# Moving the b2 add of seven batches off TensorE, with an earlier W1 copy and a halved last store, in a one-core conditional adapter kernel

## The chip, the core and the metric

The kernel runs on one core of one Trainium2 chip. A core has five engines with an instruction queue each: TensorE (PE in the profile; its weight loads are listed as PEld), VectorE (DVE), ScalarE (ACT), GpSimd (POOL) and SyncE (SP). SyncE only issues transfers here; ScalarE issues a few as well. The engines run side by side and meet at semaphores. The metric is the device time of one execution in microseconds, the median of three runs: 309.11 us (308.94 to 309.33).

## The reference

The input x is 128 batches of 128 rows by 512 columns in float32. Each batch has a language id (0 to 8), and ten sets of parameters lie in memory. Each batch picks its own set:

```python
w1 = W1[language_ids]          # 512 x 128 for each batch
w2 = W2[language_ids]          # 128 x 512
h = jnp.einsum('bsh,bha->bsa', hidden_states, w1) + b1[language_ids][:, None, :]
h = jax.nn.relu(h)
adapted = jnp.einsum('bsa,bah->bsh', h, w2) + b2[language_ids][:, None, :]
x = hidden_states + adapted
mean = jnp.mean(x, axis=-1, keepdims=True)
var = jnp.mean(jnp.square(x - mean), axis=-1, keepdims=True)
normed = (x - mean) * jax.lax.rsqrt(var + LN_EPS)
return normed * gamma[language_ids][:, None, :] + beta[language_ids][:, None, :]
```

What this returns is added to x once more, so the result is x + normalised(x + adapted) * gamma + beta.

## The kernel before

One tile is one batch: 128 rows on the partitions, 512 columns. The work of a batch b is spread over the engines:

- TensorE: `transpose_x(b)` (line 234, four 128x128 transposes into PSUM), `down(b)` (line 257, four products with W1, printed as eight matmul records), `up(b)` (line 274, the product with W2, printed as two).
- ScalarE: `copy_xT(b)` (line 238, the transposed x out of PSUM), `relu(b)` (line 265), `stage_w1(b)` (line 225, a copy of the W1 of the batch's id out of a table in SBUF), `square(b)` (line 310, the sum of squares), `root` (line 320).
- VectorE: `residual(b)` (line 291, y + r with the row sum), `scale(b)` (line 353, subtract the mean and multiply by gamma), `finish(b)` (line 362, multiply by the reciprocal deviation and add what lies in o), and four small steps for each pair of batches (lines 298, 324, 326, 329).
- GpSimd: `add_b2(b)` (line 244, r = x + b2) and `add_beta(b)` (line 251, o = x + beta).
- SyncE: loads of x, four batches at a time (line 71), and stores of two batches (line 366).

The b2 of a batch is added in one of three ways. `b2_by_matmul` lets TensorE do it: one bf16 matmul (line 273) picks the row of b2 and writes it into PSUM ahead of the product with W2. `b2_by_vector` lets VectorE add it into PSUM (line 284) ahead of `residual`. All other batches have it from GpSimd, as r. Where TensorE or VectorE does it, `residual` reads x itself instead of r.

The order on every engine is the order in which the program is written: `keep` ties each instruction to the one before it on the same engine. The main loop runs over i; in turn i TensorE transposes batch i, multiplies `down(i - 1)` and `up(i - 2)`, and the rest works on b = i - 3.

Buffers bound how far one engine runs ahead of another. The PSUM tiles y of `up` (pool p_y) are five, so `up(b + 5)` waits for `finish(b)`. The tiles r (pool rp) are four. The tiles o hold two batches each and are five; each is free again when its store has landed. The tiles w1s (one batch's W1) are five. The transposed x in PSUM is one.

Ahead of the loop, nine matmuls on ones (`spin`) run on TensorE, then the rows of beta, gamma and b2 for all ten ids are spread over the partitions (`spread`, lines 205 to 210): 30 matmuls, each copied out of PSUM by VectorE or ScalarE.

W1 comes to a batch in three ways. Batches below FIRST (8) load it from memory by id (`load_first`, line 154). Batches from FIRST to EARLY - 1 (23) copy it out of w1e, a table in which row p * 4 + k of W1 lies on partition p; x is transposed with a matching stride. From EARLY (24) on, batches copy it out of w1, where rows k * 128 + p lie on partition p; this table is loaded by four transfers of 640 KB (`load_w1`, line 103) in turns 12, 14, 16 and 18.

The last batches (`tail`) are finished one at a time. With E = 123, GpSimd and ScalarE finish batches 123 and 124 and the left half of 125 (`by_pool`, lines 408 to 412); VectorE finishes the others (`finish_cols`, line 419). `store_last` (line 415) stores one batch; the stores of 124 and 125 are issued by ScalarE, the last one (127) by SyncE.

Of the kernel before, what the change touches and what calls it, by code (L numbers as in the profile page):

```python
# [16 lines left out]
P = 128  # L17
G = 4
EPS = 1e-5
FIRST = 8  # L20
EARLY = 24
LATE = 12
U = 2

# [2 lines left out]
def cond_resid_kernel(ctx: ExitStack, tc: tile.TileContext, x, itok, W1, b1, W2, b2, gamma, beta, out):  # L27
# [8 lines left out]
    nc = tc.nc  # L36
    B, S, H = x.shape
# [8 lines left out]
    def keep(ins):  # L46

        engine = ins.ins.engine
        if engine in last:
            tc.add_manual_dep(ins.ins, last[engine], behind, reason="kept order")  # L50
        last[engine] = ins.ins.name
        return ins
# [14 lines left out]
    E = B - 5  # L67
# [6 lines left out]
    def xb(b):  # L74
        return xs[b // G][:, b % G, :]
# [11 lines left out]
    def load_part(lo, hi):  # L87
        dst = xs[lo // G][:, lo % G : lo % G + hi - lo, :]
        keep(nc.sync.dma_start(out=dst, in_=x[lo:hi].rearrange("b s h -> s b h")))
# [11 lines left out]
    def load_w1(k):  # L101
        keep(
            nc.sync.dma_start(out=w1[:, :, k, :], in_=W1[:, k * P : (k + 1) * P, :].rearrange("l p a -> p l a"))
        )
# [28 lines left out]
    def lid(b, engine):  # L133
        g = b // G
        if (g, engine) not in lids:
            loads, vals = nc.values_load_multi_w_load_instructions(
                lang[0:1, g * G : (g + 1) * G],
                engines=[engine],
                min_val=0,
                max_val=L - 1,  # L140
                skip_runtime_bounds_check_because="clamped on the chip to 0..L-1 above",
            )
            for ins in loads:
                keep(ins)
            lids[g, engine] = vals
        return lids[g, engine][b % G]
# [4 lines left out]
    def load_first(b):  # L151
        w1s[b] = wp.tile([P, KC, A], FP, tag="w1s", name=f"w1s_{b}")
        src = W1[bass.ds(lid(b, ET.SP), 1)].rearrange("o (p k) a -> p (o k a)", k=KC)
        keep(nc.sync.dma_start(out=w1s[b].rearrange("p k a -> p (k a)"), in_=src))
# [5 lines left out]
    def load_early(lo, hi):  # L160
        dst = w1e[:, lo:hi].rearrange("p l k a -> p l (k a)")
        keep(nc.sync.dma_start(out=dst, in_=W1[lo:hi].rearrange("l (p k) a -> p l (k a)", k=KC)))
# [13 lines left out]
    xs[2] = xp.tile([P, G, H], FP, tag="x", name="x_2")  # L176
    load_part(2 * G, 2 * G + 2)
    load_early(0, 5)
    load_early(5, L)
    load_part(2 * G + 2, 3 * G)  # L180

    left = rp.tile([P, H], FP, tag="r", name="left")
# [29 lines left out]
    xT, hT, rs, os, ys, ssqs, nmeans, rstds = {}, {}, {}, {}, {}, {}, {}, {}  # L212
# [1 line left out]


    def b2_by_matmul(b):
        return b in (0, 1, 2, 3, 5, B - 1) or (b % 32 == 30 and b < E)

    def b2_by_vector(b):
        return 8 <= b < B - 8 and (b % 4 == 1 if b < 24 else b % 16 in (1, 6, 11))  # L220

    def stage_w1(b):
        w1s[b] = wp.tile([P, KC, A], FP, tag="w1s", name=f"w1s_{b}")
        src = (w1e if b < EARLY else w1).rearrange("p l k a -> p (l k a)")[:, bass.ds(lid(b, ET.Activation) * (KC * A), KC * A)]
        keep(nc.scalar.copy(w1s[b].rearrange("p k a -> p (k a)"), src))  # L225

    def transpose_x(b):
        pxs[b] = p_x.tile([P, KC, P], FP, tag="xT", name=f"pxT_{b}")
        for k in range(KC):
            if b < EARLY:  # L230
                cols = xb(b).rearrange("s (p k) -> s k p", k=KC)[:, k, :]
# [54 lines left out]
    def residual(b):  # L286
        r = rs.pop(b) if b in rs else xb(b)
        if b % 2 == 0:
            sums[b // 2] = st.tile([P, 2], FP, tag="sum", name=f"sum_{b // 2}")
        keep(  # L290
            nc.vector.scalar_tensor_tensor(ys[b], ys[b], 1.0, r, ALU.mult, ALU.add, accum_out=col(sums, b))  # L291
        )
# [76 lines left out]
    def on(b):  # L369
        return 0 <= b < B  # L370
# [26 lines left out]
    def rstd_col(b):  # L397
        return rstds[b] if b > E else rstds[b // 2][:, b % 2 : b % 2 + 1]
# [12 lines left out]
        o = os[b // 2][:, b % 2, cols]  # L411
        keep(nc.gpsimd.tensor_tensor(o, n, o, ALU.add))

    def store_last(b, engine=nc.sync):
        keep(engine.dma_start(out=out[b], in_=os[b // 2][:, b % 2, :]))

    def finish_cols(b, cols=slice(0, H)):
        o = os[b // 2][:, b % 2, cols]
        keep(nc.vector.scalar_tensor_tensor(o, ys[b][:, cols], rstd_col(b), o, ALU.mult, ALU.add))  # L419

    def tail(b):
        p = E // 2
        residual(b)
        if b == E + 1:
            rstd(p, 1)
            scale(E - 1)
            rstd(p, 2)
            finish(E - 2)
            store(p - 1)
            rstd(p, 3)  # L430
            deviation_of(b)
            shift(E)
            by_pool(E, False)
        elif b == E + 2:
            rstd_of(b - 1, 1)
            negative_means(b // 2)
            rstd_of(b - 1, 2)
            finish_cols(E - 1)
            store_last(E - 1)
            rstd_of(b - 1, 3)  # L440
            store_last(E)
            deviation_of(b)
        elif b == E + 3:
            left, right = slice(0, H // 2), slice(H // 2, H)
            shift(b - 2)
            by_pool(b - 2, False)
            residual(b + 1)
            rstd_of(b - 1, 1)
            scale(b - 1)
            negative_means(b // 2)  # L450
            rstd_of(b - 1, 2)
            deviation_of(b)
            scale(b)
            rstd_of(b - 1, 3)
            rstd_of(b, 1)
            deviation_of(b + 1)
            rstd_of(b, 2)
            finish_cols(b - 1, right)
            by_pool(b - 1, True, left)
            store_last(b - 2, nc.scalar)  # L460
            store_last(b - 1, nc.scalar)
            rstd_of(b, 3)
            rstd_of(b + 1, 1)
            finish_cols(b)
            store_last(b)
            rstd_of(b + 1, 2)
            scale(b + 1)
            rstd_of(b + 1, 3)
            finish_cols(b + 1)
            store_last(b + 1)  # L470


    def spin(n, width):
        idle = p_s.tile([P, H], FP, tag="s", name="idle")
        for _ in range(n):
            keep(
                nc.tensor.matmul(
                    idle[:, :width], lhsT=ones, rhs=ones[:, 0:1].to_broadcast([P, width]), start=True, stop=True
                )
            )  # L480


    spin(9, H)

    def spread_turn(lo, hi):
        for r in range(lo, hi):
# [28 lines left out]
    for i in range(3, B + U):  # L515
        b = i - U - 1
        if b > G and b % G == 2 and b // G + 3 < NG:
            load_x(b // G + 3)
        if i == 5:
            load_x(3)  # L520
        if i in (12, 14, 16, 18):
            load_w1((i - 12) // 2)
        if i == 4:
            up(2)
        if i == 5:
            up(3)
        if i > 3 and on(i):
            transpose_x(i)
        if b <= E:
            add_b2(b + 2)  # L530
            add_beta(b)
        if i > 4 and on(i - 1):
            down(i - 1)
        if i > 3 and on(i):
            copy_xT(i)
        if i > 4 and on(i - 1):
            relu(i - 1)
        if i + 1 >= LATE and on(i + 1):
            stage_w1(i + 1)
        if i > 5 and on(i - U):  # L540
            up(i - U)


        g, half = divmod(b, 2)
        p = g - 1
        mine, old = 0 <= p < B // 2, 0 <= p - 1 < B // 2
        if b == E:
            add_b2(b + 3)
            add_beta(b + 1)
            add_b2(b + 4)  # L550
            for n in range(b + 2, B):
                add_beta(n)
        if b > E:
            tail(b)
        elif half == 0:
            if on(b):
                vector_b2(b)
                residual(b)
            if mine:
                scale(2 * p)  # L560
                rstd(p, 1)
            if old:
                finish(2 * p - 1)
                store(p - 1)
        else:
            if on(b):
                vector_b2(b)
            if mine:
                rstd(p, 2)
            if on(b):  # L570
                residual(b)
            if mine:
                rstd(p, 3)
                scale(2 * p + 1)
            if on(b):
                negative_means(g)
            if mine:
                finish(2 * p)
        if 0 <= b <= E:
            square(b)  # L580
            if half == 1:
                deviation(g)
        if FIRST <= i + 1 < LATE:
            stage_w1(i + 1)

        for n, engine in ((i + 3, ET.Activation), (i - U + 3, ET.PE), (b + 1, ET.DVE), (b + 5, ET.Pool)):
            if on(n):
                lid(n, engine)
# [37 lines left out]
```

## Time and profile before

| what | value |
|---|---|
| median of three runs | 309.11 us (308.94 to 309.33) |
| the profiled execution, its own time | 308.95 us |
| its span, first to last instruction | 307.19 us |
| TensorE busy | 296.1 us (96%) |
| VectorE busy | 294.7 us (96%) |
| ScalarE busy | 280.5 us (91%) |
| GpSimd busy | 284.4 us (93%) |
| moved by DMA | 77.59 MB, mean 253 GB/s |
| b2 matmuls on TensorE (line 273) | 9, 380 ns each by the record |
| b2 adds on VectorE (line 284) | 22, 691 ns each |
| b2 adds on GpSimd (line 244) | 97, 1289 ns each |
| beta adds on GpSimd (line 251) | 128, 1289 ns each |

A duration in the profile runs from the start of an instruction to its end. Neighbours on one engine overlap a little, so the distance from start to start is shorter than the duration; where an engine is full, that distance is its price. Busy time is counted once where instructions overlap. An idle time is given with what ended it; "issue" means that the trace shows nothing that the engine waited for. A queue name such as SPq or ACTq stands for an engine that issues transfers.

### The profile page before, as it was taken

To read this page: it belongs to the slowest core of one execution; us is meant where nothing else is said; L and a number is where in the kernel's file an instruction comes from. 1 tells how busy PE (TensorE), PEld (TensorE's weight loads), DVE (VectorE), ACT (ScalarE), POOL (GpSimd) and SP (SyncE) were. 2 spreads that over 40 slices of the span, in tenths; PEclk is the share of its full clock that TensorE was granted. 3 is DMA by queue.
4 is the path that set the end of the run, shared out by engine and by line. 5 is a ranking of instruction groups with operands and counts; after the bars stand their busy time and mean duration, and the time that the engine had idled before them with its cause. 6 is when DMAs were issued, how large, how long until landed. Compare 5 with 4: busy or idle time off the path is not lost. (4 is left out here: it accounts for less than half of the span.)

```text
span 307.2 us, 6980 instructions
## 1 busy us (share of the span) xinstructions
PE 296.1 (96%) x1841; PEld 220.6 (72%) x1841; DVE 294.7 (96%) x825; ACT 280.5 (91%) x716; POOL 284.4 (93%) x238
## 2 busy tenths in 40 slices
PE   8999999999999999999999999999999999999970
PEld 3757778777777777777777777777777777777740
DVE  6877999999999999999999999999999999999994
ACT  3858999999999999999999999999999999999982
POOL 1349999998999999999999999999999999999994
PEclk9999999999999999999999999999999999999995
DMA  6999969986777667767876676777767666782244
GB/s 233 390 389 385 384 221 369 358 300 229 247 274 265 219 205 227 254 230 247 274 265 211 195 234 247 249 248 274 237 222 235 223 237 221 276 273 109 110 160 171
DMA packets 43481, 77.59 MB, mean 253 GB/s; under 512 B 1929, under 2 KB 7060, under 8 KB 43442
## 3 DMA queue, kind: packets, MB, share of 16 engines
q1 hardware_dynamic: 43094, 76.57, 72.2%
q10 hardware_dynamic: 348, 0.57, 0.5%
q8 instruction: 15, 0.25, 0.3%
q14 instruction: 24, 0.20, 0.2%
HBM read 43.58 MB, written 33.55 MB: 251 GB/s over the span
## 5 line engine op out<-in xcount | busy, mean ns | idle before, releaser
L251 POOL TENSOR_TENSOR o<-x,beta_b 128x512 f32<-128x512 f32 x128 | 163.4, 1289 | 9.5 <-DVE beta_b L210 9.5
L257 PE MATMUL ph<-xT,w1s 128*128 128x128 f32 x1024 | 135.3, 275 | 0.0
L244 POOL TENSOR_TENSOR r<-x,b_b 128x512 f32<-128x512 f32 x97 | 125.0, 1289 | 8.5 <-DVE b_b L210 6.2
L274 PE MATMUL py<-w,hT 128*128 x256 | 131.2, 594 | 0.0
L257 PEld LDWEIGHTS ph<-xT,w1s 128*128 128x128 f32 x1024 | 124.9, 192 | 1.0 <-ACT hT L265 0.5
L234 PEld LDWEIGHTS pxT<-ident,x 128*128 128x128 f32 x512 | 66.5, 152 | 66.0 <-issue 32.1
L353 DVE SCALAR_TENSOR_TENSOR py<-py,nmean,gamma_b 128x512 f32<-128x512 f32 x126 | 95.0, 754 | 0.0
L310 ACT ACTIVATE sq<-py,sum 128x512 f32<-128x512 f32 x124 | 86.3, 696 | 5.4 <-DVE nmean L298 2.4
L362 DVE SCALAR_TENSOR_TENSOR o<-py,rstd,o 128x512 f32<-128x512 f32 x122 | 90.9, 745 | 0.0
L234 PE MATMUL pxT<-ident,x 128*128 128x128 f32 x512 | 78.5, 276 | 0.0
L238 ACT COPY xT<-pxT 128x512 f32<-128x512 f32 x128 | 74.7, 584 | 3.9 <-PE pxT L234 3.9
L291 DVE SCALAR_TENSOR_TENSOR py<-py,r 128x512 f32<-128x512 f32 x97 | 67.1, 692 | 1.4 <-PE py L274 1.2
L225 ACT COPY w1s<-w 128x512 f32 x104 | 64.1, 616 | 0.0
L265 ACT ACTIVATE hT<-ph,b1T 128x128 f32<-128x128 f32 x128 | 47.3, 370 | 4.9 <-PE ph L257 2.5
L274 PEld LDWEIGHTS py<-w,hT 128*128 128x128 f32 x256 | 39.4, 192 | 1.8 <-issue 0.9
L310 ACT ACTIVATION_READ_ACCUMULATOR sq<-py,sum 128x1 f32 x124 | 25.4, 205 | 0.0
L291 DVE SCALAR_TENSOR_TENSOR py<-py,x 128x512 f32<-128x512 f32 x31 | 21.6, 698 | 1.6 <-issue 0.8
L320 ACT ACTIVATE root<-ssq,eps 128x2 f32<-128x2 f32 x62 | 16.5, 265 | 2.1
L284 DVE TENSOR_TENSOR py<-py,b_b 128x512 f32<-128x512 f32 x22 | 15.2, 691 | 0.1
L291 DVE DVE_READ_ACCUMULATOR py<-py,r 128x1 f32 x97 | 13.8, 142 | 0.0
L225 ACT COPY w1s<-w1e 128x512 f32 x16 | 9.8, 611 | 1.1 <-DMA w1e<-in_L_cond_W_dram 1.1
L324 DVE SCALAR_TENSOR_TENSOR part<-ssq,root 128x2 f32<-128x2 f32 x62 | 9.4, 151 | 0.9 <-ACT root L320 0.8
(54 smaller groups left out, 96.1 us busy)
## 6 DMA issues: line engine op xcount, KB each, us to landing
out_dram<-o SPq DMA_DIRECT2D x61, 512.0 KB, 3.3
x<-in_x_dram SPq DMA_DIRECT2D x29, 1024.0 KB, 6.4
x<-in_x_dram SPq DMA_DIRECT2D x6, 512.0 KB, 8.9
w1e<-in_L_cond_W_dram SPq DMA_DIRECT2D x2, 1280.0 KB, 11.7
w<-in_L_cond_W_dram SPq DMA_DIRECT2D x4, 640.0 KB, 7.4
w1s<-in_L_cond_W_dram SPq DMA_DIRECT2D x8, 256.0 KB, 8.2
w<-in_L_cond_W_dram SPq DMA_DIRECT2D x1, 1792.0 KB, 10.1
out_dram<-o SPq DMA_DIRECT2D x4, 256.0 KB, 2.0
```

Source lines behind the costliest of these rows:

```text
L225: keep(nc.scalar.copy(w1s[b].rearrange("p k a -> p (k a)"), src))
L234: keep(nc.tensor.transpose(pxs[b][:, k, :], cols, ident))
L238: keep(nc.scalar.copy(xT[b], pxs.pop(b)))
L244: keep(nc.gpsimd.tensor_tensor(rs[b], xb(b), b2_b[:, bass.ds(v * H, H)], ALU.add))
L251: keep(nc.gpsimd.tensor_tensor(os[g][:, j, :], xb(b), beta_b[:, bass.ds(v * H, H)], ALU.add))
L257: nc.tensor.matmul(phs[b], lhsT=w1s[b][:, k, :], rhs=xT[b][:, k, :], start=(k == 0), stop=(k == KC - 1))
L265: keep(nc.scalar.activation(hT[b], phs.pop(b), AF.Relu, bias=b1T[:, bass.ds(lid(b, ET.Activation), 1)]))
L274: keep(nc.tensor.matmul(ys[b], lhsT=hT[b], rhs=w2[:, bass.ds(v * H, H)], start=not m, stop=True))
L291: nc.vector.scalar_tensor_tensor(ys[b], ys[b], 1.0, r, ALU.mult, ALU.add, accum_out=col(sums, b))
L310: nc.scalar.activation(sq, ys[b], AF.Square, bias=col(sums, b), scale=-float(H), accum_out=col(ssqs, b))
L353: nc.vector.scalar_tensor_tensor(ys[b], ys[b], col(nmeans, b), gamma_b[:, bass.ds(v * H, H)], ALU.add, ALU.mult)
L362: nc.vector.scalar_tensor_tensor(o, ys.pop(b), rstds[g][:, j : j + 1], o, ALU.mult, ALU.add)
```

## The change

Five things change. The b2 of batches 0 to 3, 5 and 94 is added by VectorE instead of TensorE, and that of batch 62 by GpSimd; TensorE keeps 30 and 127. A ninth batch (8) loads its W1 by id; this load stands between the two halves of w1e in SyncE's queue, and ScalarE's copy for batch 8 goes. The regular table w1 is loaded in turns 8, 10, 12 and 14, and is used from batch 21. The store of batch 127 is halved: VectorE finishes the left 256 columns and SyncE stores them, then VectorE finishes the right ones and ScalarE stores them. And a tenth spin of half the width follows the nine.

```diff
-FIRST = 8
-EARLY = 24
+FIRST = 9
+EARLY = 21
...
     load_early(0, 5)
+    load_first(2 * G)
     load_early(5, L)
...
     def b2_by_matmul(b):
-        return b in (0, 1, 2, 3, 5, B - 1) or (b % 32 == 30 and b < E)
+        return b in (30, B - 1)
 
     def b2_by_vector(b):
-        return 8 <= b < B - 8 and (b % 4 == 1 if b < 24 else b % 16 in (1, 6, 11))
+        return b < 4 or b in (5, 94) or 8 <= b < B - 8 and (b % 4 == 1 if b < 24 else b % 16 in (1, 6, 11))
...
-    def store_last(b, engine=nc.sync):
-        keep(engine.dma_start(out=out[b], in_=os[b // 2][:, b % 2, :]))
+    def store_last(b, engine=nc.sync, cols=slice(0, H)):
+        keep(engine.dma_start(out=out[b][:, cols], in_=os[b // 2][:, b % 2, cols]))
...
-            finish_cols(b + 1)
-            store_last(b + 1)
+            for cols, engine in ((left, nc.sync), (right, nc.scalar)):
+                finish_cols(b + 1, cols)
+                store_last(b + 1, engine, cols)
...
     spin(9, H)
+    spin(1, H // 2)
...
-        if i in (12, 14, 16, 18):
-            load_w1((i - 12) // 2)
+        if i in (8, 10, 12, 14):
+            load_w1((i - 8) // 2)
```

## The prediction

> **What bounds the kernel now.** I read the busy time by stretch first (columns: stretch, length, then busy time and instruction count of PE, PEld, DVE, ACT, POOL, then granted clock, DMA share, GB/s).
>
> ```profile
> 20.00:30.00 10.00, 10.00 (x55) 7.29 (x54) 7.52 (x22) 7.02 (x18) 10.00 (x9) 1.00 1.05 388
> 30.00:40.00 10.00, 10.00 (x64) 7.58 (x63) 9.24 (x26) 8.88 (x24) 9.31 (x8) 1.00 0.87 329
> 40.00:290.00 250.00, 250.00 (x1595) 190.04 (x1594) 249.76 (x706) 242.44 (x627) 248.40 (x203) 1.00 0.72 245
> ```
>
> From 40 to 290 us TensorE, VectorE and GpSimd are all full: VectorE is idle for 0.24 us, GpSimd for 1.60. Spare VectorE time lies only between 20 and 40 us: 2.48 + 0.76 = 3.24. The next view, order of time, shows TensorE's beat around batch 62 and GpSimd around 67 us.
>
> ```profile
> 152.90 1.02 PE L274 MATMUL py<-w,hT 128*128 x2
> ...
> 155.13 0.38 PE L273 MATMUL py<-parts,pick 96*128 96x512 bf16 x1
> 155.35 1.02 PE L274 MATMUL py<-w,hT 128*128 x2
> ...
> 157.54 1.02 PE L274 MATMUL py<-w,hT 128*128 x2
> ```
>
> An ordinary batch takes 157.54 - 155.35 = 2.19 us of TensorE; the b2 matmul adds 155.35 - 155.13 = 0.22.
>
> ```profile
> 67.26 1.29 POOL L251 TENSOR_TENSOR o<-x,beta_b 128x512 f32<-128x512 f32 x1
> 69.91 1.28 POOL L244 TENSOR_TENSOR r<-x,b_b 128x512 f32<-128x512 f32 x1 [1.36 <-DVE py L291]
> 71.15 2.51 POOL L251 TENSOR_TENSOR o<-x,beta_b 128x512 f32<-128x512 f32 x2
> ```
>
> GpSimd goes at 1.23 us an operation (71.15 to 73.62 for two). Here it had run as far ahead as its four r buffers let it: r of batch 26 waits until VectorE has read r of batch 22 at 69.09. The waits from 40 to 290 us list 1.6 us for this, in two stops (the other, 0.3 us, near 118); after that GpSimd never stops again until the tail:
>
> ```profile
> 297.27 1.29 POOL L410 TENSOR_TENSOR n<-n,gamma_b 128x512 f32<-128x512 f32 x1
> 298.64 1.27 POOL L412 TENSOR_TENSOR o<-n,o 128x512 f32<-128x512 f32 x1
> 299.87 1.26 POOL L410 TENSOR_TENSOR n<-n,gamma_b 128x512 f32<-128x512 f32 x1
> 301.21 1.95 POOL L412 TENSOR_TENSOR o<-n,o 128x512 f32<-128x512 f32 x2
> 302.51 1.05 ACTq L415 DMA_DIRECT2D out_dram<-o  x2
> 302.72 0.75 DVE L419 SCALAR_TENSOR_TENSOR o<-py,rstd,o 128x512 f32<-128x512 f32 x1
> ```
>
> The n of batch 123 was ready at 295.55 + 0.78 = 296.33 and waited until 297.27 for the last beta add. GpSimd's own queue therefore sets the stores of batches 124 and 125 on ScalarE's queue (GpSimd ends at 303.16), as VectorE sets the last store (303.47). Then the transfers:
>
> ```profile
> 303.00:304.00 1.00, 0.00 (x0) 0.00 (x0) 0.47 (x1) 0.00 (x0) 0.16 (x1) 0.50 0.96 363
> 304.00:305.00 1.00, 0.00 (x0) 0.00 (x0) 0.00 (x0) 0.00 (x0) 0.00 (x0) 0.50 1.02 385
> 305.00:306.00 1.00, 0.00 (x0) 0.00 (x0) 0.00 (x0) 0.00 (x0) 0.00 (x0) 0.50 0.48 184
> ```
>
> Three stores of 256 KB (0.79 MB, 2.05 us at 385 GB/s) run back to back, from about 303.35 (0.84 after the first was issued) to about 305.5; some 1.65 us of landing and closing follow to 307.19. The printed chain of waits ends in VectorE's last operations and does not show that the last store queued behind the two of ScalarE.
>
> **TensorE.** Seven b2 matmuls leave: 7 x 0.22 = 1.54 us. Batches 21 to 23 move from the strided layout to the regular one: the beat is 2.22 us from batch 10 to 21 and 2.19 from 22, so 3 x 0.03 = 0.09 more. At the head this serves as follows: without the b2 of batches 0 to 3 and 5, up(8) comes some 5 x 0.22 = 1.1 us sooner. All of this is worth only what VectorE and GpSimd can follow, since both are full.
>
> **VectorE.** An add into PSUM (line 284) costs a wait besides itself, for residual must see its result. Residual to residual over two batches: 51.22 to 55.35 = 4.13 without an add; 64.29 to 69.09 = 4.80 with one on an odd batch (0.67); 99.56 to 104.42 = 4.86 on an even one (0.73). Batch 1 has no small step between add and residual, so it counts as even: 3 x 0.73 + 2 x 0.67 = 3.53 us at the head, 0.73 at batch 94. What hides the 3.53 are the idle 3.24 us. Each of some ten gaps also hides the overlap of neighbours (a scale takes 0.75, its successor starts after 0.66), about 0.8 in all, making 4.0; 0.3 of that, around the first negative mean, is dependency and stays. VectorE also starts sooner: up(0) takes the place of its b2 matmul, 0.2. So at batch 9 it is ahead by g = 4.0 - 0.3 - 3.53 + 0.2 = 0.4 us. Without the overlap part and the early start it is 3.24 - 0.3 - 3.53 = -0.6; with every gap filled 0.7. Batch 94 comes where nothing is idle: -0.73. VectorE's last operation moves by -0.4 + 0.73 = +0.3, and by 0.13 more since it is halved (the 128x256 form took 483 ns, its successor started 0.40 on, against 0.75 whole).
>
> **GpSimd.** Batch 62 adds 1.23 us to a queue with no stop behind it. In front of it lie the two stops, and both are waits for VectorE's residual, so they shorten only as far as VectorE is ahead. One thing comes later: x of batches 10 and 11, for which GpSimd waited until 32.69, is issued behind one more W1 of 256 KB (0.26 MB / 0.388 = 0.7 us), to 33.4; GpSimd would then reach r of batch 26 at 68.5 + 0.7 = 69.2, still before VectorE frees its buffer at 69.91 - 0.4 = 69.5. So GpSimd's end moves by 1.23 - g = 0.8 us, between 1.23 - 1.1 = 0.1 (own work alone, both stops gone) and 1.8. The r are ready 4.6 to 9 us before VectorE reads them, so nobody in the middle sees this; the tail does.
>
> **The W1 loads.** The ninth by id takes a copy (line 225, 616 ns) off ScalarE and ends its wait of 1.1 us for w1e near 31 us; ScalarE has room, 0 on the path; uncovered, it would be those 1.7 us of gain at the head, all of which only feed TensorE. On SP it adds a register load, a move and a DMA that waits for down(3), done by 17.2 us, with transfers saturated (1.05) until 38: no hole, but w1e's second half, x of 10 and 11 and x of 12 to 15 land 0.7 later. The four copies of 640 KB move ahead of x of 16 to 19, of the stores of pairs 1 to 3 and of x of 20 to 23. They fill the hole at 38 to 40 us (68 GB/s). The last is issued behind the fourth store (before: 44.4) instead of at 53.8, and with its 8.9 us it lands by 54, where batch 21 is copied near 59. A store that lands late holds GpSimd's o buffer (five pairs): the fourth store landed 6.0 us after 44.4, and its buffer is wanted at 51.2. One 640 KB copy more in front is 1.7 us at worst, so 0 to 0.9 on GpSimd; I take 0, since these issues also come about 1 us sooner.
>
> **The extra spin** costs TensorE 0 to 0.2 (half of the 0.43 between spins) if x of batch 0 has landed by 5.1 us; I take 0. The granted clock is given as 1.00 throughout, yet nine spins took 4.02 us (0.45 each) while seven row matmuls of the same width took 1.78 (0.25), so the head starts slow. [...]
>
> **The end.** The left half of batch 127 goes out on SP at about 303.5, beside the other stores. The right half queues on ScalarE behind the two stores that wait for GpSimd. After the store of batch 125 (issued at 303.2 + 0.8 = 304.0, flowing 0.84 later for 0.68) only 128 KB are left (0.34): 304.0 + 0.84 + 0.68 + 0.34 = 305.9 against 305.5 before: +0.3 with the rounding undone (0.83 - 0.49). [...]
>
> **Sum** against the profiled execution (308.95 us, span 307.19): +0.3. Its time stands 0.16 under the median of three, 309.11, so the forecast for the median is 309.4. Its own range, from GpSimd's bounds (0.1 - 0.5 to 1.8 - 0.5), is 308.7 to 310.4. Within 0.2% (0.62 us: 308.5 to 309.7) this kernel can't be told from no change.
>
> **Rivals.**
> Faster: *TensorE is the bound after all* and the lead of r swallows batch 62. For it speaks the rigid 2.19 us beat and VectorE's 1.7 us of waits in the tail; against it the 0.94 us for which n of batch 123 waited for GpSimd. It decides if GpSimd's tail can be late by 0.8 us unseen. 1.54 + 0.09 less 0.4 for the unfilled rest of VectorE: 309.11 - 1.2 = 307.9.
> Slower: *VectorE can't fill its head gaps.* The gaps are waits for up and for the root of the variance, and the adds lengthen just those chains (up, add, residual, square, root). finish(b) then frees its PSUM buffer later, up(b + 5) waits (its margin in the trace shrinks to 0.2 us by batch 61), and nothing later regains it. If 1.3 us of the gaps stay open, g = -0.9: 309.11 + (1.23 + 0.9 - 0.5) = 310.7; it is slower for certain once g falls below about 0.1.
> Slower, smaller: *the copies hold a store*, hence an o buffer, for 0.5 us: 309.9.
> Doing nothing at all is excluded: the instructions are gone from TensorE.
>
> **Chances.** Forecast 0.46 (0.37 of it within 0.2%, 0.09 above), faster rival 0.22 (0.01 within), VectorE rival 0.20, late store 0.12 (0.05 within). Faster 0.21, same 0.43, slower 0.36. Range 308.3 to 310.6: it leaves out most of the faster rival and a part of the VectorE one.
>
> **What would show it.** Right: r of batch 26 starts near 69.5, GpSimd runs from there to about 304.0 without a stop, residual of 9 lies 0.4 us ahead, up(b + 5) starts right behind finish(b) after batch 62, and the last bytes follow the store of 125. Wrong: VectorE shows new idle before 40 us (the slower rival), GpSimd stops in the middle and still ends by 303.2 (the faster one), or GpSimd stops for a DMA between 45 and 60 us (the late store).

## The result and the profile after

Timed together in seven runs each, the changed kernel takes a median of 309.76 us (309.32 to 310.46) and the kernel before 309.07 us (308.94 to 309.33). The ratio is 1.0024, with a 95% interval of 1.0013 to 1.0036: slower by 0.69 us, a difference clear of the noise but only just above 0.2%. The prediction had +0.3 us.

| profiled execution | before | after |
|---|---|---|
| its own time | 308.95 us | 309.67 us |
| its span | 307.19 us | 307.9 us |
| TensorE busy | 296.1 us | 295.0 us |
| VectorE busy | 294.7 us | 297.9 us |
| GpSimd busy | 284.4 us | 285.5 us |
| residual of batch 9 starts | 40.20 us | 39.27 us |
| residual of batch 22 starts | 69.09 us | 68.16 us |
| last operation of VectorE ends | 303.47 us | 303.34 us |
| last addition of GpSimd ends | 303.16 us | 304.35 us |

The last two rows hold the case. VectorE took on six additions and ends no later; GpSimd took on one and ends 1.19 us later.

The busy time by stretch of the changed kernel (columns as before the change):

```profile
20.00:30.00 10.00, 9.67 (x60) 7.30 (x59) 9.86 (x27) 7.61 (x20) 10.00 (x9) 1.00 1.05 387
30.00:40.00 10.00, 9.66 (x61) 7.31 (x60) 9.94 (x31) 8.71 (x24) 7.94 (x8) 1.00 1.06 376
40.00:290.00 250.00, 249.90 (x1587) 188.66 (x1586) 249.61 (x704) 240.85 (x624) 248.98 (x203) 1.00 0.72 244
```

VectorE's third column was 7.52 and 9.24 in the first two stretches; it is 9.86 and 9.94. The additions of batches 0 to 3 and 5 went into its gaps nearly whole. TensorE, which was at 10.00 in both, now has 0.33 and 0.34 us to spare there. GpSimd, which was at 9.31 between 30 and 40 us, is at 7.94. And still VectorE's residual of batch 9 comes sooner. In the kernel before:

```profile
40.20 0.70 DVE L291 SCALAR_TENSOR_TENSOR py<-py,x 128x512 f32<-128x512 f32 x1
```

In the changed kernel:

```profile
39.27 0.70 DVE L292 SCALAR_TENSOR_TENSOR py<-py,x 128x512 f32<-128x512 f32 x1
```

Where GpSimd stops, from its timeline in the changed kernel (start, duration, line, form, and in brackets the idle time ahead of it and what ended it):

```profile
33.41 1.28 POOL L245 TENSOR_TENSOR r<-x,b_b 128x512 f32<-128x512 f32 x1 [2.06 <-DMA x<-in_x_dram]
...
50.82 1.30 POOL L245 TENSOR_TENSOR r<-x,b_b 128x512 f32<-128x512 f32 x1
...
53.03 1.28 POOL L252 TENSOR_TENSOR o<-x,beta_b 128x512 f32<-128x512 f32 x1 [0.92 <-DMA out_dram<-o]
...
70.30 1.29 POOL L245 TENSOR_TENSOR r<-x,b_b 128x512 f32<-128x512 f32 x1
```

And the same summed up, its waits from 20 to 290 us (total, times, longest):

```profile
POOL r L245 <- DVE b_b L211: 6.2, 1, 6.2
POOL r L245 <- DMA x<-in_x_dram: 2.1, 1, 2.1
POOL o L252 <- DMA out_dram<-o: 0.9, 1, 0.9
```

x of batches 10 and 11 comes at 33.41 instead of 32.69. At 53.03 the beta addition of batch 16 waits 0.92 us for a buffer o whose store has not landed; the kernel before had no such stop. The two waits for VectorE's residual (1.6 us in all) are gone: GpSimd comes to r of batch 26 at 70.30, when VectorE has freed its buffer long since. So from 53 us on GpSimd never stops, and whatever was late there is late at the end. SyncE's queue shows what the late store stood behind (SPq rows are issuing instructions; their duration is how long SyncE was held by them):

```profile
40.44 1.03 SPq L103 DMA_DIRECT2D w<-in_L_cond_W_dram  x1
41.57 2.81 SPq L71 DMA_DIRECT2D x<-in_x_dram  x1
44.47 1.17 SPq L367 DMA_DIRECT2D out_dram<-o  x1
```

The store at 44.47 is that of the fourth pair (batches 6 and 7). It is issued behind a 640 KB copy of W1 and 1 MB of x, and its buffer comes free at 53.03, 8.6 us on. In the kernel before the same store was issued at 44.39, and its buffer was free in time:

```profile
41.28 0.76 SPq L71 DMA_DIRECT2D x<-in_x_dram  x1
44.39 0.38 SPq L366 DMA_DIRECT2D out_dram<-o  x1
```

So the store leaves no sooner than before, although VectorE had finished what it stores at 42.68 + 0.75 = 43.43, against 43.62 + 0.74 = 44.36 before:

```profile
42.68 0.75 DVE L363 SCALAR_TENSOR_TENSOR o<-py,rstd,o 128x512 f32<-128x512 f32 x1
```

For a microsecond it waited in SyncE's queue behind the issue of x, which held SyncE for 2.81 us instead of 0.76. What held that issue the trace does not show. Then it took 8.6 us to land, where the prediction had 6.0 from the kernel before.

The tail, in order of time:

```profile
298.47 1.28 POOL L411 TENSOR_TENSOR n<-n,gamma_b 128x512 f32<-128x512 f32 x1
...
302.40 1.95 POOL L413 TENSOR_TENSOR o<-n,o 128x512 f32<-128x512 f32 x2
302.46 0.88 DVE L420 SCALAR_TENSOR_TENSOR o<-py,rstd,o 128x256 f32<-128x256 f32 x2
...
303.69 1.55 ACTq L416 DMA_DIRECT2D out_dram<-o  x3
```

GpSimd begins its tail at 298.47 instead of 297.27 (1.20 later) and ends at 302.40 + 1.95 = 304.35; VectorE is done at 303.34, a microsecond sooner. The last store queues on ScalarE behind the one that waits for GpSimd. What the transfers do meanwhile (the last two columns are DMA share and GB/s):

```profile
303.00:304.00 1.00, 0.00 (x0) 0.00 (x0) 0.34 (x1) 0.00 (x0) 1.00 (x2) 0.50 0.50 188
304.00:305.00 1.00, 0.00 (x0) 0.00 (x0) 0.00 (x0) 0.00 (x0) 0.34 (x1) 0.50 0.63 231
305.00:306.00 1.00, 0.00 (x0) 0.00 (x0) 0.00 (x0) 0.00 (x0) 0.00 (x0) 0.50 1.00 371
306.00:307.00 1.00, 0.00 (x0) 0.00 (x0) 0.00 (x0) 0.00 (x0) 0.00 (x0) 0.50 0.37 125
```

From 303 to 305 us the DMA share is only 0.50 and 0.63: the stores that wait for GpSimd are not issued before 303.69; before, the share was 0.96 and 1.02 and transfers ran at 363 and 385 GB/s in these two stretches. They end near 306.4 instead of 305.5.

The theory to be tested: GpSimd's queue alone sets the end, and batch 62 is its largest addition. Its rivals: VectorE pays for its six adds; the W1 copies do it through the late store; the halved last store or the extra spin does it.

### The profile page after: what moved, and what is told of

Its sections match the earlier page's. It is cut to its first block, busy times and chain, and to the rows that moved or that the text cites. A ratio compares the mean times of both kernels' runs of the same rounds, so it can differ in the third digit from the quotient of the medians.

```text
span 307.9 us, 6973 instructions
## 1 busy us (share of the span) xinstructions
PE 295.0 (96%) x1835; PEld 219.0 (71%) x1835; DVE 297.9 (97%) x832; ACT 279.1 (91%) x715; POOL 285.5 (93%) x239
## 4 chain that ended last, share of the span: by engine, by line
PE 32%; POOL 31%; issue 18%; DVE 12%; POOLq 2%; DVEq 1%; ACT 1%; ACTq 0%
POOL o L252 18%; PE ph L258 12%; POOL r L245 12%; PE py L275 11%; PE pxT L235 6%; DVE py L292 5%; DVE py L354 3%; PE row L206 2%; DVE o L363 2%; DVE py L285 2%; PE idle L479 1%; POOLq L136 1%; DVEq L136 1%; POOL n L411 1%; POOL o L413 1%
## 5 line engine op out<-in xcount | busy, mean ns | idle before, releaser
L252 POOL TENSOR_TENSOR o<-x,beta_b 128x512 f32<-128x512 f32 x128 | 162.6, 1281 | 9.9 <-DVE beta_b L211 8.8
L245 POOL TENSOR_TENSOR r<-x,b_b 128x512 f32<-128x512 f32 x98 | 125.5, 1281 | 8.2 <-DVE b_b L211 6.2
L235 PEld LDWEIGHTS pxT<-ident,x 128*128 128x128 f32 x512 | 65.4, 151 | 67.5 <-ACT xT L239 37.7
L226 ACT COPY w1s<-w 128x512 f32 x107 | 66.2, 618 | 0.0
L285 DVE TENSOR_TENSOR py<-py,b_b 128x512 f32<-128x512 f32 x28 | 19.4, 692 | 0.7 <-PE py L275 0.6
L299 DVE SCALAR_TENSOR_TENSOR nmean<-sum,py 128x2 f32<-128x2 f32 x64 | 10.0, 156 | 0.1
L330 DVE SCALAR_TENSOR_TENSOR rstd<-part,root 128x2 f32<-128x2 f32 x62 | 9.4, 151 | 0.0
```

Source lines behind the costliest of these rows:

```text
L235: keep(nc.tensor.transpose(pxs[b][:, k, :], cols, ident))
L245: keep(nc.gpsimd.tensor_tensor(rs[b], xb(b), b2_b[:, bass.ds(v * H, H)], ALU.add))
L252: keep(nc.gpsimd.tensor_tensor(os[g][:, j, :], xb(b), beta_b[:, bass.ds(v * H, H)], ALU.add))
```

## The experiments

Every kernel ran beside the kernel before on the same chip. Three groups were timed, and the median of the kernel before differs between them: 308.86 us in the group of a1 to a4, 308.88 in that of b1 to b4, 309.13 in that of c1 to c4. Each difference below is against the median of its own group. The ratios' intervals reach some 0.1% (0.3 us) to each side, and the changed kernel was timed in a group of its own, so steps below about 0.3 us are read from the traces, not from the medians. The a, c and b3 kernels start from the changed kernel, the other b kernels from the kernel before. G is the end of GpSimd's last addition, V that of VectorE's last operation, in the profiled execution.

| kernel | median less before's | ratio (95%) | G | V | residual of 9 | GpSimd's stop for a store (ends at) |
|---|---|---|---|---|---|---|
| before |  |  | 303.16 | 303.47 | 40.20 | none |
| changed | +0.69 | 1.0024 (1.0013 to 1.0036) | 304.35 | 303.34 | 39.27 | 0.92 (53.03) |
| a1: 62 back | +0.20 | 1.001 (1.0001 to 1.0019) | 303.12 | 303.52 | 39.38 | 0.62 (52.47) |
| a2: W1 timing back | +0.53 | 1.0013 (1.0 to 1.0026) | 303.70 | 303.82 | 39.76 | none |
| a3: both back | +0.40 | 1.0015 (1.0006 to 1.0024) | 304.11 | 304.48 | 39.95 | 1.12 (61.65) |
| a4: both and 94 back | -0.41 | 0.9988 (0.9979 to 0.9997) | 302.40 | 302.86 | 39.28 | none |
| b1: before, extra spin | -0.05 | 0.9999 (0.999 to 1.0008) | 302.96 | 303.30 | 40.09 | none |
| b2: before, 62 on GpSimd | +0.95 | 1.003 (1.0019 to 1.0041) | 304.38 | 303.57 | 40.25 | none |
| b3: whole last store | +1.02 | 1.0024 (1.0014 to 1.0034) | 304.78 | 303.22 | 39.30 | 1.32 (53.57) |
| b4: before, head adds | +0.20 | 1.0005 (0.9996 to 1.0014) | 303.50 | 303.87 | 40.34 | 0.36 (60.38) |
| c1: 62 and 94 back | -0.43 | 0.9991 (0.9982 to 1.0) | 302.89 | 303.35 | 39.79 | 0.76 (52.77) |
| c2: 94 back | +0.42 | 1.0015 (1.0006 to 1.0024) | 304.34 | 303.10 | 39.54 | 0.82 (53.10) |
| c3: no extra spin | +0.45 | 1.0014 (1.0005 to 1.0023) | 304.10 | 303.54 | 39.48 | 0.80 (52.87) |
| c4: eight W1 by id | +0.74 | 1.0025 (1.0016 to 1.0034) | 304.07 | 304.29 | 40.20 | 0.84 (52.22) |

### b2: batch 62 on GpSimd, alone

```diff
-        return b in (0, 1, 2, 3, 5, B - 1) or (b % 32 == 30 and b < E)
+        return b in (0, 1, 2, 3, 5, B - 1) or (b in (30, 94))
```

> The kernel before with the b2 of batch 62 moved from TensorE to GpSimd and nothing else. Theory (GpSimd's queue sets the end): GpSimd ends 1.2 us later, near 304.4; the last whole store no longer queues behind those of batches 124 and 125 but ends before them, so about 0.35 us of this is not seen: 309.9 us (309.6 to 310.3). Rival (the lead of r hides it, TensorE gains): 308.8 to 309.1.

One b2 moved from TensorE to GpSimd, nothing else, costs 0.95 us: as much as the whole change, and more. In its trace from 40 to 290 us GpSimd still waits for VectorE, 1.9 us against 1.6 before:

```profile
POOL r L244 <- DVE py L291: 1.9, 2, 1.4
```

These waits take nothing from the added work. Its tail:

```profile
302.43 1.95 POOL L412 TENSOR_TENSOR o<-n,o 128x512 f32<-128x512 f32 x2
```

It ends at 304.38, or 1.22 later than before: one operation at 1.23. VectorE moved by 0.10 (303.57). Of this 1.22 us the profiled execution shows 1.07 (310.02 us against 308.95), so 0.15 of it is not seen and not the 0.35 of the expectation; whether the last store ended ahead of the other two stays open. The first of the rivals' mechanisms, VectorE's adds, is not in this kernel at all.

### a1: batch 62 back on TensorE

```diff
-        return b in (30, B - 1)
+        return b in (30, 62, B - 1)
```

> The changed kernel with the b2 of batch 62 given back to TensorE and nothing else. Theory (GpSimd's queue sets the end): GpSimd loses one operation of 1.23 us with no stop behind it, its last add ends near 303.1 instead of 304.35, the transfers after it 1.0 us sooner: 308.8 us (308.5 to 309.1). Rival (TensorE and VectorE set the end): TensorE gains 0.22 us of work, VectorE nothing: 309.8 to 310.0.

The difference falls from +0.69 to +0.20. GpSimd's waits from 40 to 290 us, and the tail:

```profile
POOL r L245 <- DVE py L292: 0.7, 1, 0.7
POOL o L252 <- DMA out_dram<-o: 0.6, 1, 0.6
```

```profile
301.17 1.95 POOL L413 TENSOR_TENSOR o<-n,o 128x512 f32<-128x512 f32 x2
302.64 0.88 DVE L420 SCALAR_TENSOR_TENSOR o<-py,rstd,o 128x256 f32<-128x256 f32 x2
```

G falls by 1.23, from 304.35 to 303.12, though only 0.49 us come off the median: now VectorE, at 303.52, is last. A wait for VectorE is back in the middle (0.7 us). Both ends lie within 0.05 us of the kernel before, for all the work that has left TensorE.

### c2 and c1: batch 94 back, and 62 with it

c2:

```diff
-        return b in (30, B - 1)
+        return b in (30, 94, B - 1)
...
-        return b < 4 or b in (5, 94) or 8 <= b < B - 8 and (b % 4 == 1 if b < 24 else b % 16 in (1, 6, 11))
+        return b < 4 or b == 5 or 8 <= b < B - 8 and (b % 4 == 1 if b < 24 else b % 16 in (1, 6, 11))
```

> The changed kernel with the b2 of batch 94 alone back on TensorE. It takes 0.73 us off VectorE and nothing off GpSimd. Theory (GpSimd's queue sets the end): no change, 309.5 to 309.9 us, though VectorE's last half ends 0.7 us sooner, near 302.6. Rival (VectorE sets the end): 309.0 to 309.1.

c1 is the same with `return b in (30, 62, 94, B - 1)`.

> The changed kernel with the b2 of batches 62 and 94 both back on TensorE, all else as changed. Theory: GpSimd loses 1.23 us and VectorE 0.73 us, so both ends move: GpSimd's last add near 302.4 to 302.6, VectorE's near 302.8: 308.3 us (308.0 to 308.6), below both kernels. Rival (TensorE's 0.44 us more counts): 309.2 or more.

This pair parts the two engines. The tail of c2:

```profile
302.22 0.88 DVE L420 SCALAR_TENSOR_TENSOR o<-py,rstd,o 128x256 f32<-128x256 f32 x2
302.40 1.94 POOL L413 TENSOR_TENSOR o<-n,o 128x512 f32<-128x512 f32 x2
```

and of c1:

```profile
300.95 1.94 POOL L413 TENSOR_TENSOR o<-n,o 128x512 f32<-128x512 f32 x2
302.47 0.88 DVE L420 SCALAR_TENSOR_TENSOR o<-py,rstd,o 128x256 f32<-128x256 f32 x2
```

In c2 GpSimd ends at 304.34, where it ended in the changed kernel, and VectorE at 303.10, 1.24 us before it. The profiled time is 309.66 us against 309.67: what VectorE gained is not to be seen in it. (The medians differ by 0.27, within what they can tell.) The test is weaker than it was meant to be: VectorE ends 0.24 us sooner than in the changed kernel and not 0.7, in part because in this execution the residual of batch 9 stands 0.27 later. In c1 GpSimd ends 1.45 us sooner than in c2, at 302.89, and the median falls by 0.85 us to 0.43 under the kernel before (308.70 us; expected were 308.0 to 308.6). With 62 on TensorE, 94 counts by the medians: a1 to c1 gives 0.63, and a3 to a4, within one group, 0.81, against the 0.73 of an add. In the traces V moves by only 0.17 from a1 to c1, since the residual of batch 9 stands 0.41 later in c1. So each engine's own end decides, and which one is last depends on where the other additions lie.

### a2 and a3: the timing of W1

a2:

```diff
-EARLY = 21
+EARLY = 24
...
-        if i in (8, 10, 12, 14):
-            load_w1((i - 8) // 2)
+        if i in (12, 14, 16, 18):
+            load_w1((i - 12) // 2)
```

> The changed kernel with the four 640 KB copies of W1 back in turns 12 to 18 and the regular table used from batch 24 again. Theory: the store of the fourth pair lands in time, GpSimd's stops for it (0.98 us at 52 us and 0.17 at 43) go, nothing behind them takes them back, GpSimd ends near 303.2: 308.7 us (308.4 to 309.1). Rival: the stops are hidden behind the lead of r: 309.8.

a3 is a2 and a1 together.

> Both of these at once. Theory: GpSimd would end 2.4 us sooner, near 302.0, ahead of VectorE, whose last half ends at 303.3 as now; VectorE then sets the end: 308.0 us (307.7 to 308.5), less than the two gains added up (307.6). Rival: 309.9.

Neither came out as the theory had it: a2 takes 309.39 us and a3 309.26. In a2 the stop for the store is gone, but the difference from the kernel before is only 0.16 smaller. GpSimd's waits for VectorE from 40 to 290 us are back in its place:

```profile
POOL r L245 <- DVE py L292: 0.8, 2, 0.5
```

GpSimd was early enough to meet its own four buffers again, and of the 0.92 us only 0.65 are left at its end (303.70). VectorE ends 0.48 later than in the changed kernel (303.82), and is then last. Its residual of batch 9 is 0.49 late already: in this execution the first transposes began at 5.43 instead of 5.00 us. In a3 GpSimd waits for a store all the same, with the old timing of W1:

```profile
POOL o L252 <- DMA out_dram<-o: 1.1, 1, 1.1
POOL r L245 <- DVE py L292: 0.9, 1, 0.9
```

The store here is a later one (the stop ends at 61.65), and the head is late again (5.43).

The last column of the table settles more than the medians. All seven kernels with the W1 copies in turns 8 to 14 stop for a store between 52.2 and 53.6 us, for 0.62 to 1.32 us, c4 without the ninth load by id among them; of the seven with turns 12 to 18 none stops there. Three pairs among them differ in nothing but the W1 timing (changed and a2, a1 and a3, c1 and a4). So the early copies are what makes that stop. In all seven the issue of x ahead of the fourth store holds SyncE for 2.75 to 2.81 us; in the other seven it is 0.76 to 2.20. But to be rid of the stop pays only in part: without it GpSimd waits for VectorE and, in a3 and b4, for a store at 60 to 62 us as well. What makes that one late was not tested. In the medians the W1 timing can't be told from nothing: -0.16 for a2 against the changed kernel, +0.20 for a3 against a1, +0.02 for a4 against c1.

### a4: W1 timing, 62 and 94 back

```diff
-EARLY = 21
+EARLY = 24
...
-        return b in (30, B - 1)
+        return b in (30, 62, 94, B - 1)
...
-        return b < 4 or b in (5, 94) or 8 <= b < B - 8 and (b % 4 == 1 if b < 24 else b % 16 in (1, 6, 11))
+        return b < 4 or b == 5 or 8 <= b < B - 8 and (b % 4 == 1 if b < 24 else b % 16 in (1, 6, 11))
...
-        if i in (8, 10, 12, 14):
-            load_w1((i - 8) // 2)
+        if i in (12, 14, 16, 18):
+            load_w1((i - 12) // 2)
```

> As the one before, with the b2 of batch 94 also back on TensorE. Theory: VectorE, now the bound, loses 0.73 us from batch 94 on, and GpSimd is still ahead: 307.4 us (307.1 to 307.9). If TensorE were the bound by then, its 0.22 us more would make it 0 to 0.2 us slower than the one before.

At 308.45 us (308.12 to 309.11) it misses the expected range by half a microsecond, but it is 0.41 under the kernel before; c1, the same with the new W1 timing, is 0.43 under its own. What is left of the change in both is the head: five additions on VectorE, the ninth W1 by id, the halved store and the spin. These two alone come out ahead of the kernel before by 0.1%, and the interval of c1 just reaches 1.0. Which part of the head earns it was not taken apart.

### b4: the head's additions on VectorE, alone

```diff
-        return b in (0, 1, 2, 3, 5, B - 1) or (b % 32 == 30 and b < E)
+        return b == B - 1 or (b % 32 == 30 and b < E)
...
-        return 8 <= b < B - 8 and (b % 4 == 1 if b < 24 else b % 16 in (1, 6, 11))
+        return b < 4 or b == 5 or 8 <= b < B - 8 and (b % 4 == 1 if b < 24 else b % 16 in (1, 6, 11))
```

> The kernel before with the b2 of batches 0 to 3 and 5 on VectorE and nothing else. Theory: VectorE's 3.5 us fit into its gaps before 40 us, residual of batch 9 stands 0.1 to 0.4 us sooner; GpSimd's stop at 67 us shortens by as much: 308.7 to 309.1 us. Rival (VectorE can't fill the gaps): residual of batch 9 later by 0.5 us or more, 309.6 or more.

Neither the theory nor its rival came true. The residual of batch 9 comes at 40.34, not ahead of 40.20, nor 0.5 us late as the rival had it. V is 0.40 later than before, and the median, 309.08 us, is 0.20 above the kernel before, which its interval does not tell from nothing. ScalarE, from its timeline:

```profile
31.43 0.62 ACT L225 COPY w1s<-w1e 128x512 f32 x1 [2.12 <-DMA w1e<-in_L_cond_W_dram]
```

and VectorE:

```profile
33.80 0.16 DVE L324 SCALAR_TENSOR_TENSOR part<-ssq,root 128x2 f32<-128x2 f32 x1 [0.30 <-ACT root L320]
...
35.20 0.70 DVE L291 SCALAR_TENSOR_TENSOR py<-py,r 128x512 f32<-128x512 f32 x1 [0.51 <-PE py L274]
...
40.34 0.70 DVE L291 SCALAR_TENSOR_TENSOR py<-py,x 128x512 f32<-128x512 f32 x1
```

ScalarE stands 2.12 us in front of the copy of batch 8's W1, because w1e has not landed; the squares and the next products stand behind it, and VectorE has gaps of 0.30 and 0.51 us for them. But the additions are not the reason. The same wait stands in b1, which has none of them there:

```profile
31.17 0.62 ACT L225 COPY w1s<-w1e 128x512 f32 x1 [1.62 <-DMA w1e<-in_L_cond_W_dram]
```

In all five kernels with eight W1 by id this copy waits for w1e (at 31.29 us before, 31.17 in b1, 31.35 in b2, 31.43 in b4, 31.29 in c4), and in all five the residual of batch 9 starts 8.90 to 8.92 us after it, with the additions or without. So the additions fit into VectorE's gaps here too, but they bring nothing ahead, because the landing of w1e sets when batch 9 comes.

### c4: eight W1 by id

```diff
-FIRST = 9
+FIRST = 8
...
-    load_first(2 * G)
```

> The changed kernel with batch 8 taking its W1 from w1e again, the ninth load by id gone. x of batches 10 and 11 lands 0.7 us sooner (GpSimd goes on at 32.7 instead of 33.4), but ScalarE waits for w1e near 31 us again and VectorE keeps gaps of 0.4 and 0.6 us near 33 and 35, residual of batch 9 at 40.3 instead of 39.3. Theory: GpSimd's stop for r comes back for what the earlier x gives, VectorE ends near 304.4: 309.6 to 309.9 us. Rival (the ninth load is what made the changed kernel slower): 309.0.

The other side of the same thing: ScalarE waits again, for 1.89 us.

```profile
31.29 0.62 ACT L225 COPY w1s<-w1e 128x512 f32 x1 [1.89 <-DMA w1e<-in_L_cond_W_dram]
```

The x of batches 10 and 11 is back at 32.68, 0.73 sooner, so that load is what delays it. But the residual of batch 9 falls back from 39.27 to 40.20, and V from 303.34 to 304.29. GpSimd gets 0.28 of it at its end and VectorE loses 0.95; the median stays (+0.74 against +0.69). In the nine kernels that have the ninth load this wait is gone, and the residual of batch 9 starts 33.45 to 33.57 us after the first four transposes end, whatever else differs. So with the ninth load the start of the head sets when batch 9 comes, and without it the landing of w1e. The ninth load without the additions was not tried.

### b3: the last store whole

```diff
-            for cols, engine in ((left, nc.sync), (right, nc.scalar)):
-                finish_cols(b + 1, cols)
-                store_last(b + 1, engine, cols)
+            finish_cols(b + 1)
+            store_last(b + 1)
```

> The changed kernel with the last store whole again, by SyncE. In the changed kernel the right half queues behind the two stores that wait for GpSimd. Theory: the whole store goes out at about 303.3 on SyncE, flows from 304.0 and is nearly through when the store of 124 begins to flow at 304.5; the 128 KB behind the store of 125 are gone: 309.4 us (309.2 to 309.6). Rival (the halving helps): 309.9 to 310.2.

Inconclusive: the median, 309.90 us, lies outside the expected range and at the rival's, but in the profiled execution GpSimd waited 1.32 us for a store and ended 0.43 later than in the changed kernel. The traces can be compared by the time that is left after the end of the engine that ends last (the execution's own time less V or G). Where VectorE is last by 0.3 us or more, that is 5.43 to 5.48 us with the store whole (before, b1, b4) and 5.26 to 5.35 with the store halved (a1, a3, a4, c1). This is about 0.15, or what VectorE pays for its two halves (0.13). In a2 and c4, also halved, GpSimd ends within 0.22 us of VectorE, and it is 5.58 and 5.57. Where GpSimd is last, whole gives 5.13 (b3) and 5.64 (b2), halved 5.32 (changed, c2) and 5.39 (c3). These are single executions; what the halving saves or costs stays open.

### b1 and c3: the spin

b1 adds the spin to the kernel before, c3 takes it from the changed one.

```diff
     spin(9, H)
+    spin(1, H // 2)
```

> The kernel before with the extra half spin alone. In the changed kernel's profile the first transposes took 0.72 us instead of 1.10 and everything up to the first up stood 0.7 us sooner. Theory A (the spin closes the idle stretch before the first transpose and TensorE is at full clock sooner, every time): first residual 0.7 us sooner, and since the stop of GpSimd at 67 us shortens as VectorE gains: 308.4 to 308.6 us. Theory B (where the clock rises is chance from run to run): no change in the median, 308.9 to 309.2. Theory C (it only delays): 309.3.

> The changed kernel without the extra half spin. Theory: when TensorE's clock rises is chance from run to run, and where it rises late the spin only holds the first transpose back, from 5.10 to 5.43 us; since GpSimd is held by transfers in the head, little of it reaches the end: 309.5 to 309.8 us. Rival (the spin brings the clock sooner and VectorE's lead with it): 310.0 or more, first transposes 1.1 us in the profile.

b1 is at -0.05, c3 0.24 below the changed kernel, and neither can be told from nothing. The first instructions of TensorE, in b1:

```profile
1.19 4.01 PE L477 MATMUL idle<-ones 128*128 128x512 bf16 x10 [1.19 <-POOL ones L111]
5.09 0.72 PE L234 MATMUL pxT<-ident,x 128*128 128x128 f32 x4
```

in c3:

```profile
1.18 4.02 PE L479 MATMUL idle<-ones 128*128 128x512 bf16 x9 [1.18 <-POOL ones L111]
5.17 0.86 PE L235 MATMUL pxT<-ident,x 128*128 128x128 f32 x4
```

and in a3:

```profile
1.19 4.45 PE L479 MATMUL idle<-ones 128*128 128x512 bf16 x10 [1.19 <-POOL ones L111]
5.43 1.06 PE L235 MATMUL pxT<-ident,x 128*128 128x128 f32 x4
```

Ten spins take 4.01 us in one and 4.45 in another; the four transposes behind them 0.72 and 1.06. Nine spins are followed by 0.86 here, 1.10 in the kernel before and 0.72 in b2 and b4. Whether the head starts quickly differs from one kernel's execution to another's, with or without the tenth spin; where the ten spins run slowly they hold the transposes back, to 5.43 in a2, a3 and c1 and 5.37 in c2.

## Why the prediction was right or wrong

The bound and the direction were right and the range held the time; of the size, +0.69 us, less than half had been forecast (+0.3). That GpSimd's move came as near as it did (0.8 forecast, 1.19 measured) is in part luck: terms that the sum left out or had wrong made up for each other.

- **GpSimd's queue sets the end.** Shown: b2 moves one addition there and pays 0.95 us; a1 takes it back and G falls by 1.23; in c2 VectorE ends 0.24 sooner, G stays, and so does the profiled time. The faster rival, with TensorE as the bound, is out: TensorE has less to do and the kernel is slower.
- **The tail formula**, GpSimd's move less 0.49, gave the right number. With the G that came, 1.19 - 0.49 = 0.70; the profiled executions are 0.72 apart. Part of this is luck: the transfers ended 0.9 later than before (306.4 against 305.5), and only because what follows the last of them took 1.5 us instead of 1.7 do 0.7 remain. They ended 0.5 later than the 305.9 forecast, of which 0.35 is GpSimd.
- **The failed term: the late store, taken at 0.** The stop that its rival named (0.5 us, chance 0.12) came, at 0.92 us, just beyond the 0.9 given as its bound. The reason for the 0 was that "these issues also come about 1 us sooner", and that failed: the data were ready 0.93 sooner, but SyncE was held by the issue of x and issued the fourth store at 44.47, 0.08 later than before. The store then held its buffer for 8.6 us where 6.0 had been assumed. In c4, where the data are as late as before and the store is issued at 44.39, it still takes 7.8, so the late issue is not the whole of it. That the early W1 copies make this stop is shown by seven kernels with them against seven without. What it costs in time is less than its length: a2, without it, is only 0.65 us sooner at G and 0.16 in the median.
- **GpSimd's sum** then reads: 1.23 for batch 62, 0.72 for x of 10 and 11 (forecast 0.7), 0.92 for the store, 0.17 for one more short stop near 43 us, less 1.36 and 0.24 for the two waits that are gone: 1.44, against 1.19 measured; the mean addition of 1281 ns instead of 1289 points the same way, and the rest stays open. The forecast was 0.8. Its lower bound, 0.1 with both stops gone, took off 1.1 us without saying from where: the stops were 1.60, both went, and the end still moved by 1.19. Its statement that r of batch 26 would start near 69.5 was wrong; it started at 70.30: GpSimd, late by then, no longer met VectorE there, so nothing of g reached it.
- **VectorE's head.** The direction was right, g = 0.4 too small: residual of 9 is 0.93 ahead. Part of this is chance, the quick start of TensorE in this execution: where the first transposes were held to 5.43, g was 0.25 (a3), 0.41 (c1) and 0.44 (a2). The first four transposes ended at 5.72 in the changed kernel and at 6.20 before; with the start of the kernel before, and the 33.5 us from their end to the residual of batch 9, g would have been about 0.5 (an estimate: 40.20 - 39.7), near the forecast. With g = 0.93 the forecast's own terms give -0.93 + 0.73 + 0.13 = -0.07 for VectorE's end, against -0.13 measured.
- **The ninth load by id, "0 on the path", was the wrong step about the head.** b4 and c4 show that without it ScalarE waits for w1e, and batch 9 comes 8.9 us after that wait, at 40.34 and 40.20, as it did before: g is 0 or a little less. So the load, put at 0, is the condition of the whole lead. It is worth some 0.9 us to VectorE (c4) and costs GpSimd 0.7 by delaying x. The rival "VectorE can't fill its head gaps" is not borne out, with the load or without it: even in b4, g is -0.14 and not -0.9.
- **Batch 94, -0.73 on VectorE.** Near, by the medians: 0.63 (a1 to c1) and 0.81 (a3 to a4), where VectorE is last. In the changed kernel it lies under GpSimd's later end and is not seen in the profiled time (c2), as the sum, made from GpSimd alone, had it; c2's VectorE ended only 0.24 sooner, so this is a weak test.
- **The spin**, 0: nothing in the runs speaks against it. That a clock rises, sooner or later, as the theories for b1 and c3 have it, no run shows: the granted clock is 1.00 from 0 to 10 us before and after the change. What the runs show is the time of the first four transposes, 0.71 us (c2) to 1.10 (before). **The halved store**: its right half is issued last (at 304.8 us), behind the stores that wait for GpSimd, as the sum had it, and lands 2.0 us on; what the halving adds or saves stays open. That up(b + 5) would start right behind finish(b) after batch 62 shows in the changed kernel in two places only: at 229 and 236 us up waited for finish, 0.16 and 0.29 us.

## What to carry to other kernels

When three engines are full, a piece of work moved from one to another is priced at the end of each engine's own queue: here 1.23 us of one addition gave 0.95 us of time, while an addition taken off an engine that ends a microsecond earlier (c2) gave nothing in the profiled time. Ask of each move which engine ends last with it, and try the parts alone and in pairs; the useful part of this change (what a4 and c1 keep, some -0.4 us, barely above what can be told) was hidden by two additions in full stretches. Ask also what an engine will wait for once its gap is filled: here the gain at the head was held by one transfer, and more work taken away ahead of it brought nothing ahead (b4: residual of batch 9 at 40.34 us against 40.20). A load put in early to free one engine delayed what another waited for (x of batches 10 and 11, by 0.73 us), and copies issued ahead of a store in a stretch full of transfers (DMA share 1.08 from 44.5 to 53 us) came back as a buffer that the late store held (stops of 0.62 to 1.32 us).

## What the runs showed of the hardware

- A store of a pair held its buffer far longer than its bytes take: 8.6 us from issue in the changed kernel for 512 KB, which at the 385 GB/s reached from 304 to 305 us before the change would flow in 1.4 us (an estimate: 0.52 MB / 0.385). Which store is late differs: with the early copies GpSimd's stop ended at 52 to 54 us, without them there was none, or one at 60 to 62 (a3, b4).
- An issuing instruction held its engine: that of x ahead of the fourth store took SyncE 2.81 us in the changed kernel and 0.76 before, and the store behind it left a microsecond after its data were ready (44.47 against 43.43).
- TensorE's first matmuls were slow, and when they got faster differed between executions: after the same nine spins the four first transposes took 0.72 us (b2, b4), 0.86 (c3) and 1.10 (before), where the four of the next batch took 0.63 (before, from 7.45 us). The profile's granted clock is 1.00 from 0 to 10 us all the same (before, changed); what makes the difference no run shows.
- A quick start gained little where a transfer set the pace behind it: b1's four transposes end 0.39 us sooner than those of the kernel before (5.81 against 6.20), but its residual of batch 9 comes only 0.11 sooner (40.09 against 40.20), since ScalarE then waited 1.62 us for w1e instead of 1.05.
- Whether the two queues of the halved store save anything no run here shows: from VectorE's end, where it is last, to the end of the execution it was 5.26 to 5.58 us with them (a1 to a4, c1, c4) and 5.43 to 5.48 without (before, b1, b4).
